# Four quarter sums in an attention kernel: standing together, or spread over v's block products

## The chip, the cores and the metric

The kernel runs on one core of a Trainium2 chip. The metric is the device time of one execution in microseconds; before the change its median over three runs is 3327.03 us (3325.53 to 3331.03). The engines are named as the profile names them: PE is TensorE (PEld its weight loads), DVE is VectorE, ACT is ScalarE, POOL is GpSimd and SP is SyncE, which issues the DMAs. Everything is in fp32.

## The reference

Two layers run one after the other on an input of 8 batches, 512 channels and 32 x 32 points (1024 tokens). Layer 0 is a group norm, an attention of 8 heads, an output projection with a second group norm, and a residual. Layer 1, in which the change lies, is an attention of one head over all 512 channels with weights normalised by row:

```python
def _L1_conv_ref(x, v_qkv, g_qkv, v_out, g_out):
    ...
    qkv = jnp.einsum('oc,bcn->bon', w_qkv, xt)
    rms = jnp.sqrt(jnp.mean(jnp.square(qkv), axis=1, keepdims=True)) + 0.0001
    qkv = qkv / rms
    q, k, v = jnp.split(qkv, 3, axis=1)
    scores = jnp.einsum('bci,bcj->bij', q, k) * C ** (-0.5)
    attn = jax.nn.softmax(scores, axis=-1)
    h = jnp.einsum('bij,bcj->bci', attn, v)
    h = jnp.einsum('oc,bcn->bon', w_out, h).reshape(B, C, H, W)
    return (x + h) * 2.0 ** (-0.5)
```

## The kernel before

The kernel loops over the 8 batches. For each it does layer 0 (`Heads`, then `finish_layer0` or, for the last batch, `finish_last`) and then layer 1 (`Layer1`, lines 739 to 907). The end of layer 1 of one batch is woven into the beginning of layer 0 of the next.

Layer 1 never forms q and k. Weights are multiplied together ahead of the loop, so that with the normalised input x of the layer the scores are x-transposed times u, where u is the product of the prepared matrix `score` with x, and v (already multiplied by the output weights) is the product of x with the prepared matrix `value`. The scale by the root mean square is put on afterwards: u's columns are multiplied by a row `rrow` on GpSimd (line 803), v's rows by `rinv` on ScalarE (line 823).

The three large products of the layer, u, v and e (the exponentials of the scores), are made by the class `Seven` (lines 607 to 689): a product of two by two blocks with seven block multiplications instead of eight (Strassen and Winograd's form). It needs, beside the blocks themselves, four sums and differences of the left operand's blocks, S1 to S4, and four of the right one's, T1 to T4. In `Seven.steps` the order of the seven is

```python
for a, b, drain in (
    (A11, "B11", c11_first),
    (S2, "T2", lambda pm: add(c["12"], c["11"], pm)),
    (S3, "T3", c22_first),
    (A22, "T4", c21),
    (S1, "T1", both),
    (S4, "B22", c12),
    (A12, "B21", c11),
):
    self.product(a, b, drain)
    yield
```

Each `product` is two matmuls of 128 contracted rows that accumulate in one PSUM bank; on the chip each fp32 matmul is two matmul instructions, so a product is four of them. Two products share one wide tile of the pool `ps_s` (three buffers of two banks each, line 101): the class variable `Seven.half` holds the second half until the next product takes it, also across units. When both halves are filled, the additions that take the two products out of PSUM ("drains", line 641) are given to VectorE, or to ScalarE for the copy `c11_first`. So additions come after every second product.

Layer 1's part of a batch, in `Layer1.project`, runs in this order: the products with `gram` and the root mean square; two units (m = 0, 1) of u's products, with x's sums T1 to T4 made on VectorE; four units of v's (line 875, each product of 256 columns); four units of e's (line 881, 512 columns). For e's the left operand is u, whose sums S1 to S4 are `s12` and `s34`, made by `sum_u` (line 830) on VectorE from u's quarters: four operations over 128 x 1024 elements. They can begin only when GpSimd has scaled u, and `sum_u` is called after v's second unit (line 877). `sum_u` also creates the tiles for the sums (pool `prob`, two buffers) and takes two of the large slots for e.

The order of the work on each engine is the order of the program text: `InOrder` (line 26) pins every instruction to it. So whatever stands ahead in an engine's queue and waits holds up what stands behind it. The tile framework adds the semaphore waits between engines. Every instruction is issued through line 34, so the profile's lines all read L34, and one tells instructions apart by their tiles. The profile leaves numbers out of tile names: `s` is `s12` or `s34` where it is next to u or in a 128x1024 addition of two tensors (it is also the name of layer 0's scores), `t` is a tile of T sums, `p_u_B`, `p_v_T`, `p_e_B` and so on are the PSUM tiles of u's, v's and e's units, named after the first letter of the right operand of the pair's first product, B or T.

Of the kernel before, what the change touches and what calls it, by code (L numbers as in the profile page):

```python
# [52 lines left out]
def attention_blocks_kernel(  # L53
# [50 lines left out]
    PE, VE, AC, PO, SY = (InOrder(tc, e) for e in (nc.tensor, nc.vector, nc.scalar, nc.gpsimd, nc.sync))  # L104

    def big(name, lead=CI):

        return slots.take([P, lead, CI * N // lead], name)
# [14 lines left out]
    def run(pieces):  # L123
        for _ in pieces:
            pass
# [95 lines left out]
    def place(name, b):  # L221
        tag, shape = places[name]
        near[name] = weights.tile(shape, F32, tag=f"w_{tag}", name=f"{name}_{b}")
        if name == "v":

            flat = near[name].rearrange("p k h c -> p (k h c)")
            near["v#"] = flat[:, CI * C :]
            near[name] = flat[:, : CI * C].rearrange("p (ci c) -> p ci c", ci=CI)
        return near[name]

    def fetch(name, b):
        SY.dma_start(out=place(name, b), in_=far[name])
# [506 lines left out]
    class Layer1:  # L739
# [10 lines left out]
        def project(self):  # L750
# [41 lines left out]
            u = self.u = big(f"u_{b}")  # L792
# [22 lines left out]
            def value_unit(m):  # L815

                w = near["value"]
                c = {f"{i + 1}{th + 1}": v[:, m + 4 * th, i * CH : (i + 1) * CH] for i in range(2) for th in range(2)}

                def last(which):  # L820
                    if which[0] == "1":
                        t = m + 4 * (which == "12")
                        AC.activation(v[:, t, :], v[:, t, :], AF.Copy, scale=rinv[:, t : t + 1])

                return Seven(
                    f"v_{b}_{m}", CH,
                    lambda k, h: w[:, k, h, :], self.right(slice(m * P, (m + 1) * P)), c, last, swap=True,
                )

            def sum_u():  # L830

                s12 = prob.tile([P, 2, 2, HN], F32, tag="p", name=f"s12_{b}")
                s34 = prob.tile([P, 2, 2, HN], F32, tag="p", name=f"s34_{b}")
                q1, q2 = halves_
                VE.tensor_add(s12[:, 0], u[:, :2, q2], u[:, 2:, q2])
                VE.tensor_sub(s12[:, 1], s12[:, 0], u[:, :2, q1])
                VE.tensor_sub(s34[:, 0], u[:, :2, q1], u[:, :2, q2])
                VE.tensor_sub(s34[:, 1], u[:, 2:, q1], s12[:, 1])
                self.s12, self.s34 = s12, s34
                for th in range(2):  # L840
                    e[th] = big(f"e_{b}_{th}", NT)
                    self.sums[th] = sum_pool.tile([P, HN], F32, tag="esum", name=f"esum_{b}_{th}")

            def weight_unit(m):

                def left(k, h):
                    if k in (A11, A12, A22):
                        return u[:, 2 * (k != A11) + h, halves_[k == A22]]  # L850
                    return {S1: self.s12[:, 0], S2: self.s12[:, 1], S3: self.s34[:, 0], S4: self.s34[:, 1]}[k][:, h, :]

                c = {f"{th + 1}{i + 1}": e[th][:, m + 4 * i, :] for i in range(2) for th in range(2)}

                def last(which):
                    th, t = int(which[0]) - 1, m + 4 * (int(which[1]) - 1)
                    et, esum = c[which], self.sums[th]
                    AC.activation(et, et, AF.Exp, bias=shift, scale=rinv[:, t : t + 1])
                    done[th].append(et)
                    if len(done[th]) == 2:  # L860
                        PO.tensor_add(esum, *done[th])
                    elif len(done[th]) > 2:
                        PO.tensor_add(esum, esum, et)

                return Seven(f"e_{b}_{m}", HN, left, self.right(slice(m * P, (m + 1) * P)), c, last, swap=True)
# [6 lines left out]
                        broadcast()  # L872
            if b + 1 < B:
                fetch("qk", b + 1)
            for m in range(4):
                run(value_unit(m).steps())
                if m == 1:
                    sum_u()
            if b + 1 < B:
                fetch("v", b + 1)  # L880
            for m in range(4):
# [139 lines left out]
    for b in range(B):  # L1021
        hn, more = heads.hn, b + 1 < B
        todo = iter(())
        for i in range(STEPS):
# [18 lines left out]
            if more:  # L1043
# [9 lines left out]
                k = i - 3 * CI - 2  # L1053
# [97 lines left out]
```

## Time and profile before

| | us |
|---|---|
| median of three runs (lowest, highest) | 3327.03 (3325.53, 3331.03) |
| the profiled execution | 3326.53 |
| its span, first to last instruction | 3324.7 |
| granted TensorE clock, mean over the span | 0.997 |
| additions into s12 and s34, 16 that read u alone | 19.5, 1218 ns each |
| the same, 8 with s first (s<-s,u) | 9.8, 1225 ns each |
| the same, 8 with s last (s<-u,s) | 9.7, 1218 ns each |
| additions into v from PSUM, 160 from p_v_T | 64.5, 420 ns each |
| additions into v from PSUM, 64 from p_v_B | 25.4, 417 ns each |
| GpSimd's scaling of u, 64 | 78.9, 1270 ns each |
| ScalarE's scaling of v, 64 | 43.6, 716 ns each |
| matmul instructions of v's products, 448 + 320 + 64 + 64 | 379 to 382 ns each |

The profile is of one execution. A page gives busy time by engine, and views of the same trace give groups of like instructions, waits, and the instructions in order of time. In the timeline a line is: start, duration, engine, line, operation, the tile written and the tiles read, shape, the number of like instructions merged, and in square brackets how long the engine was idle before it and what ended that. Matmuls overlap one another: one of 256 columns is shown with 379 ns, while 16 of them in a row start within 3.45 us. The time between starts is therefore the measure, not the sum of durations.

### The profile page before, as it was taken

To read this page: it belongs to the slowest core of one execution; us is meant where nothing else is said; L and a number is where in the kernel's file an instruction comes from. 1 tells how busy PE (TensorE), PEld (TensorE's weight loads), DVE (VectorE), ACT (ScalarE), POOL (GpSimd) and SP (SyncE) were. 2 spreads that over 40 slices of the span, in tenths; PEclk is the share of its full clock that TensorE was granted. 3 is DMA by queue.
4 is the path that set the end of the run, shared out by engine and by line. 5 is a ranking of instruction groups with operands and counts; after the bars stand their busy time and mean duration, and the time that the engine had idled before them with its cause. 6 is when DMAs were issued, how large, how long until landed. Compare 5 with 4: busy or idle time off the path is not lost.

```text
span 3324.7 us, 35644 instructions
## 1 busy us (share of the span) xinstructions
PE 3270.4 (98%) x13189; PEld 1608.1 (48%) x13189; DVE 2127.5 (64%) x2893; ACT 1069.8 (32%) x1811; POOL 981.4 (30%) x855
## 2 busy tenths in 40 slices
PE   7999999999999999999999999999999999999799
PEld 3544544445444454444544445444544445444354
DVE  4596646965479554885449754596646965478653
ACT  2353123521245212451215412254123531245210
POOL 0253123521245112450224503254123521234111
PEclk9999999999999999999999999999999999999899
DMA  5586205751068410782118811387204752067400
GB/s 187 160 212 189 76 13 155 195 176 67 7 185 209 147 45 26 204 224 95 45 50 217 236 47 44 88 216 199 76 13 142 200 166 93 5 159 203 151 7 25
DMA packets 182659, 411.86 MB, mean 124 GB/s; under 512 B 27444, under 2 KB 27480, under 8 KB 176344
## 3 DMA queue, kind: packets, MB, share of 16 engines
q1 hardware_dynamic: 182368, 409.58, 43.3%
q8 instruction: 105, 1.72, 0.2%
q14 instruction: 66, 0.54, 0.0%
q10 hardware_dynamic: 120, 0.02, 0.0%
HBM read 113.53 MB, written 27.56 MB: 42 GB/s over the span
## 4 chain that ended last, share of the span: by engine, by line
PE 86%; DVE 6%; DMA 5%; SPq 2%; issue 1%; ACT 0%; DVEq 0%; POOL 0%; POOLq 0%; ACTq 0%
PE po L34 24%; PE pqk L34 11%; PE s L34 11%; PE pv L34 7%; PE p_e_T L34 7%; PE p_e_B L34 5%; DMA pT<-pb 5%; PE py L34 4%; PE p_u_T L34 3%; PE p_o_T L34 3%; PE p_v_T L34 2%; PE p_u_B L34 2%; DVE pb L34 2%; PE p_o_B L34 2%; PE p_v_B L34 2%; SPq L34 2%
## 5 line engine op out<-in xcount | busy, mean ns | idle before, releaser
L34 ACT ACTIVATE p<-s,nm 128x1024 f32<-128x1024 f32 x512 | 565.5, 1109 | 861.3 <-DVE nm L34 825.7
L34 POOL TENSOR_SCALAR p<-p,tt 128x1024 f32<-128x1024 f32 x512 | 565.9, 1118 | 927.3 <-DVE tt L34 923.9
L34 DVE TENSOR_REDUCE nm<-s 128x1 f32<-128x1024 f32 x512 | 602.6, 1219 | 176.3 <-PE s L34 175.1
L34 DVE STREAM_TRANSPOSE pb<-p 128x2048 f32<-128x2048 f32 x256 | 589.6, 2303 | 23.2 <-POOL p L34 18.7
L34 PE MATMUL s<-qk 64*128 64x512 f32 x2048 | 508.1, 602 | 0.0
L34 PE MATMUL po<-pT,v 128*64 128x256 f32 x4096 | 470.3, 382 | 4.1 <-DMA pT<-pb 2.6
L34 PE MATMUL pqk<-hn,qk 64*128 64x512 f32 (+1 forms) x2016 | 473.9, 591 | 0.0
L34 PE MATMUL po<-e,v 128*128 128x512 f32 x1024 | 450.9, 595 | 0.0
L34 PEld LDWEIGHTS po<-pT,v 128*64 128x64 f32 x4096 | 286.7, 137 | 216.4 <-ACT v L34 71.3
L34 PEld LDWEIGHTS pqk<-hn,qk 64*128 64x128 f32 (+1 forms) x2016 | 201.8, 187 | 252.1 <-issue 239.7
L34 PEld LDWEIGHTS po<-e,v 128*128 128x128 f32 x1024 | 192.2, 190 | 252.7 <-issue 245.5
L34 POOL TENSOR_TENSOR u<-u,xy 128x512 f32<-128x512 f32 x64 | 78.9, 1270 | 781.3 <-DMA xy<-far_rinv 781.3
L34 PEld LDWEIGHTS s<-qk 64*128 64x128 f32 x2048 | 193.3, 186 | 238.6 <-issue 235.1
L34 PE MATMUL pv<-v,hn 128*128 128x512 f32 x512 | 230.7, 602 | 1.4 <-ACT v L34 1.4
L34 DVE TENSOR_TENSOR e<-e,p_e_T 128x512 f32<-128x512 f32 x160 | 107.1, 686 | 145.0 <-PE p_e_T L34 142.8
L34 POOL TENSOR_TENSOR qk<-qk,v 128x512 f32<-128x512 f32 x124 | 158.3, 1277 | 83.9 <-ACT v L34 83.9
L34 ACT ACTIVATE e<-e,shift,rinv 128x512 f32<-128x512 f32 x128 | 100.9, 811 | 247.7 <-DVE e L34 247.7
L34 POOL TENSOR_TENSOR esum<-esum,e 128x512 f32<-128x512 f32 x96 | 121.5, 1267 | 163.9 <-ACT e L34 161.4
L34 PEld LDWEIGHTS pv<-v,hn 128*128 128x128 f32 x512 | 95.3, 191 | 117.8 <-issue 116.0
L34 PE MATMUL p_e_T<-s,t 128*128 128x512 f32 x320 | 147.8, 592 | 0.0
L34 DVE TENSOR_TENSOR v<-po,esum 128x512 f32<-128x512 f32 x56 | 38.7, 691 | 160.0 <-PE po L34 159.8
L34 PE MATMUL py<-x,gram 128*128 128x512 f32 x320 | 140.7, 599 | 0.0
(184 smaller groups left out, 3077.8 us busy)
## 6 DMA issues: line engine op xcount, KB each, us to landing
pT<-pb SPq DMA_DIRECT2D x1024, 256.0 KB, 4.6
hn<-in_x_dram SPq DMA_DIRECT2D x32, 512.0 KB, 5.5
x<-in_x_dram SPq DMA_DIRECT2D x32, 512.0 KB, 5.8
out_dram<-x SPq DMA_DIRECT2D x32, 512.0 KB, 4.0
score<-far_score SPq DMA_DIRECT2D x8, 1792.0 KB, 7.5
value<-far_value SPq DMA_DIRECT2D x8, 1792.0 KB, 7.1
qk<-far_qk SPq DMA_DIRECT2D x7, 2048.0 KB, 8.1
proj<-far_proj SPq DMA_DIRECT2D x7, 1792.0 KB, 8.4
```

The source lines that it names most:

```text
L34: return lambda *args, **kw: self._pin(call(*args, **kw))
```

## The change

`sum_u` becomes a generator. Its four VectorE operations are the same, on the same tiles and in the same order, and there is a `yield` after each of the first three. The tiles and slots are made when it is first advanced. The loop over v's four units now goes through the products one by one and advances the generator after the products (unit 2, product 0), (2, 4), (3, 1) and (3, 5), counted from zero. Nothing else differs.

```diff
@@ -832,14 +832,17 @@
                 s12 = prob.tile([P, 2, 2, HN], F32, tag="p", name=f"s12_{b}")
                 s34 = prob.tile([P, 2, 2, HN], F32, tag="p", name=f"s34_{b}")
                 q1, q2 = halves_
-                VE.tensor_add(s12[:, 0], u[:, :2, q2], u[:, 2:, q2])
-                VE.tensor_sub(s12[:, 1], s12[:, 0], u[:, :2, q1])
-                VE.tensor_sub(s34[:, 0], u[:, :2, q1], u[:, :2, q2])
-                VE.tensor_sub(s34[:, 1], u[:, 2:, q1], s12[:, 1])
                 self.s12, self.s34 = s12, s34
                 for th in range(2):
                     e[th] = big(f"e_{b}_{th}", NT)
                     self.sums[th] = sum_pool.tile([P, HN], F32, tag="esum", name=f"esum_{b}_{th}")
+                VE.tensor_add(s12[:, 0], u[:, :2, q2], u[:, 2:, q2])
+                yield
+                VE.tensor_sub(s12[:, 1], s12[:, 0], u[:, :2, q1])
+                yield
+                VE.tensor_sub(s34[:, 0], u[:, :2, q1], u[:, :2, q2])
+                yield
+                VE.tensor_sub(s34[:, 1], u[:, 2:, q1], s12[:, 1])
 
             def weight_unit(m):
 
@@ -872,10 +875,11 @@
                         broadcast()
             if b + 1 < B:
                 fetch("qk", b + 1)
+            sums = sum_u()
             for m in range(4):
-                run(value_unit(m).steps())
-                if m == 1:
-                    sum_u()
+                for k, _ in enumerate(value_unit(m).steps()):
+                    if (m, k) in ((2, 0), (2, 4), (3, 1), (3, 5)):
+                        next(sums, None)
             if b + 1 < B:
                 fetch("v", b + 1)
             for m in range(4):
```

## The prediction

> **What bounds the kernel now.** I read the page first, for the share of each engine; then the list of waits of TensorE alone, because that engine is nearly always busy; then the timeline of the first batch around the four sums, TensorE and VectorE apart; last the same timeline of other batches, to see whether it repeats.
>
> ```profile
> span 3324.7 us, 35644 instructions
> PE 3270.4 (98%) x13189; PEld 1608.1 (48%) x13189; DVE 2127.5 (64%) x2893; ACT 1069.8 (32%) x1811; POOL 981.4 (30%) x855
> ```
>
> TensorE is busy for 98% of the span, so time is won only where it stands still. Its waits (who waited for whom, us in total, times, longest):
>
> ```profile
> PE pv L34 <- DVE d L34: 16.8, 5, 5.8
> PE pcol L34 <- DMA rows<-in_L_conv_b_qkv_dram: 10.6, 1, 10.6
> PE p_v_B L34 <- DVE v L34: 5.8, 8, 0.7
> ```
>
> One of them comes eight times, once per batch: v's block products wait for VectorE's additions into v. The sums are in front of those. TensorE in the first batch:
>
> ```profile
> 405.61 3.62 PE L34 MATMUL p_v_T<-value,t 128*128 128x256 f32 x16
> 409.06 2.75 PE L34 MATMUL p_v_B<-value,x 128*128 128x256 f32 x12
> 411.65 1.03 PE L34 MATMUL p_v_B<-value,t 128*128 128x256 f32 x4
> 412.51 2.75 PE L34 MATMUL p_v_T<-value,t 128*128 128x256 f32 x12
> 415.10 1.03 PE L34 MATMUL p_v_T<-value,x 128*128 128x256 f32 x4
> 416.86 1.99 PE L34 MATMUL p_v_B<-value,x 128*128 128x256 f32 x8 [0.73 <-DVE v L34]
> 418.69 3.62 PE L34 MATMUL p_v_T<-value,t 128*128 128x256 f32 x16
> 422.15 1.89 PE L34 MATMUL p_v_B<-value,x 128*128 128x256 f32 x8
> 423.87 1.88 PE L34 MATMUL p_e_B<-u,x 128*128 128x512 f32 x4
> ```
>
> and VectorE, and GpSimd's scaling of u, in the same stretch:
>
> ```profile
> 398.50 9.86 POOL L34 TENSOR_TENSOR u<-u,xy 128x512 f32<-128x512 f32 x8 [99.02 <-DMA xy<-far_rinv]
> ...
> 410.99 0.75 DVE L34 TENSOR_TENSOR v<-v,p_v_B 128x256 f32<-128x256 f32 x2 [0.52 <-PE p_v_B L34]
> 411.66 1.22 DVE L34 TENSOR_TENSOR s<-u 128x1024 f32<-128x1024 f32 x1
> 412.98 1.23 DVE L34 TENSOR_TENSOR s<-s,u 128x1024 f32<-128x1024 f32 x1
> 414.12 1.22 DVE L34 TENSOR_TENSOR s<-u 128x1024 f32<-128x1024 f32 x1
> 415.26 1.22 DVE L34 TENSOR_TENSOR s<-u,s 128x1024 f32<-128x1024 f32 x1
> 416.39 0.41 DVE L34 TENSOR_TENSOR v<-v,p_v_B 128x256 f32<-128x256 f32 x1
> 416.91 2.19 DVE L34 TENSOR_TENSOR v<-v,p_v_T 128x256 f32<-128x256 f32 x5
> ```
>
> The reader is to see the order: the four sums hold VectorE from 411.66 to 416.39, the one addition that empties the first PSUM tile of v's third unit comes behind them and ends at 416.80, and TensorE goes on at 416.86. It had run out of PSUM: the pool of wide tiles has three buffers, each takes two products (a pair), and the fourth pair of the unit needs the first pair's buffer.
>
> **The size of the hole.** A pair is 8 matmul instructions; 16 start in 409.06 - 405.61 = 3.45 us, so a pair takes 1.73 and a product 0.864. The block of 415.10 is one product, so the next was due at 415.97; it came at 416.86, 0.89 late. The block of 416.86 takes 1.83 to the next start in place of 1.73: 0.10 more. Together 0.99. Check from outside: v's products begin at 398.70 and the next stage at 423.87, 25.17 us for 28 products worth 24.18; again 0.99. The second batch (798.49 to 823.65) gives 0.98, and the timelines of the fourth and the last show the same 0.73 idle. From 423 to 830 us this idle is the only one of TensorE's matmuls in that view, so a batch is bound by TensorE from here to the same place in the next.
>
> **What the Trainium skill says.** "PSUM — Partial Sum Buffer", section "Engine vs sequencer instructions", has VectorE's queue as strictly first in, first out; the trace agrees, since the first pair was complete at about 412.7 (ScalarE's copy out of it begins at 412.71) and its addition still stood until 416.39. "VectorE: DVE Perf Modes", section on the TRN2 errata, prices an fp32 addition of two tensors at (N+151)/0.96 ns: 1224 for 1024 elements, and the trace has 1218 to 1225. "Perfetto Trace Analysis", "Optimizing Scalar/DVE Operations", says that where VectorE isn't saturated but causes bubbles elsewhere, breaking up its work can help; that is advice, and the sum below decides. "TensorE: Matmul & The Clock Gate", "What's actually happening", lets the clock fall after about 3.4 us of idleness; the hole is shorter, and the view by windows has 1.00 throughout it, so the hole costs its own length and no slower clock.
>
> **The change part by part.** No instruction is added or removed: 4 sums per batch, 32 in all, of about 1.22 us. Creating the two tiles and taking the two slots for e moves behind one product of unit 2, issues nothing, and no other slot is taken or given there. No DMA and no GpSimd instruction moves past another; only the fetch of the next batch's weights of v, which waits for v's last product, is issued as much earlier as TensorE is.
>
> Call the pairs of units 2 and 3 A to G. With no hole they start at 410.79, 412.51, 414.24, 415.97, 417.70, 419.42 and 421.15, and the stage after at 422.88. Results reach VectorE 0.20 after a pair ends (402.16 to 402.36 in unit 0). VectorE's additions per pair, as the timeline has them: A one (0.42), B two (0.88), C three (1.21), D one, E two, F three, G two (0.75). A pair's tile is needed again two pair times after the pair ended, so its additions may end 3.45 - 0.20 = 3.25 us after they became possible. The same rule gives the hole of before: A possible at 412.71, done at 416.80, 4.09, which is 0.84 too late against 0.89 measured.
>
> Now the queue with the sums spread. The first stands where it stood: behind the additions of unit 1, since unit 2's first product gives no addition until its pair is complete. It runs 411.66 to 412.88. It waits for u's scaling, which ended at 398.50 + 9.86 = 408.36: no new wait. A's addition follows ScalarE's copy (412.71 to 413.08) and ends at about 413.5. B's two: 414.44 to 415.32. Second sum: to 416.54. C's three, possible at 416.17, are 0.4 late: to 417.75. D's: 417.9 to 418.3. Third sum: to 419.5. E's: 419.6 to 420.5. F's: 421.35 to 422.56. Fourth sum: to 423.78. G's, possible at 423.08, are 0.7 late: to 424.5, where before they ended at 424.82.
>
> Against the due times: A's tile is wanted at 415.97 and free 2.4 before; C's at 419.42, 1.7 before. D's also holds the first product of unit 3, which ScalarE copies behind two scalings of v (1.33 for two): free at about 419.5, wanted at 421.15, 1.65 before. F's is free at 422.56; the weight unit takes E's tile at 422.88 and F's at 426.3. None stalls. The sums' own readers: the second is read from 424.6 (done 416.5), the third from 426.3 (419.5), the fourth, operand S4 of the sixth product, from about 431.5 (423.8). Everything that stands behind a sum has at least 1.6 us of cover; without it the sum's lateness would be TensorE's.
>
> Sum: 8 x 0.99 = 7.9 us gained, nothing added. The profiled execution took 3326.53 (span 3324.7 and 1.83 around it): 3318.6. The median of the runs is 0.5 above it: 3319.1. Bounds of what isn't shown: a scattered sum might cost the queue 1.22 or, with the spacing of dependent sums (412.98 - 411.66), 1.32; I take 1.22, and the 0.1 is inside the cover. The removed hole can give back at most 0.99 per batch, since TensorE shows no other idle there, and at least nothing. Next late, once it is gone, is TensorE itself, matmul behind matmul.
>
> **Rivals.** First, only part goes: one buffer is still late, most likely D's through ScalarE's two scalings and copy. Half the hole left is 8 x 0.5 = 4 us gained: 3323. For it: D has the longest way out, over three engines. Against: 1.65 us of cover. Chance 0.11.
>
> Second, the microsecond is won here and lost before the batch ends, because a later wait has a clock of its own (a DMA, the normalisation chains): 3327. For it: the list has waits of TensorE for VectorE's normalisation. Against: those are five in all, mostly at the start and the last batch, and none in 423 to 830. It includes the case that the instructions come out in the old order, against which stands that every engine's order is pinned to the program's. Chance 0.07.
>
> Third, slower: VectorE falls behind for good. Units 2 and 3 load it with 5.8 of additions and 4.9 of sums in 12.1 us of products. If gaps and holds raise each scattered sum to well over twice its price, say 2.9 us, 6.7 us more come in; some 2 are absorbed by its idle time (12.1 - 10.7, and the edges), 0.7 of lateness is there already, and G, F and the first tiles of the weight unit would be 5.4 late against 3.25 and one addition of 0.75: TensorE would stand 1.4 to 2.2 us per batch, about 0.8 more than the hole: 3327 + 8 x 0.8 = 3333. It decides from about 2.4 us per sum. For it: each sum now stands ahead of two or three additions. Against: nothing in the trace has a 1024-element fp32 addition over 1.23. Chance 0.05.
>
> **The numbers.** The forecast has 0.77. The range 3315.5 to 3324.0 takes in the whole hole with the runs' spread of some 3 us, and the partial case; the last two are left out. What a measurement of this kernel can tell from no change is 0.2%, 6.7 us, and my gain of 7.9 is little above it, so a good part of the forecast's own chance falls within: faster 0.60 (about three quarters of the forecast's 0.77, and a little of nothing else), same 0.33, slower 0.07 (the third rival and the spread of the second).
>
> **What would show it.** In the changed profile: the wait of p_v_B for v gone from TensorE's list; TensorE's busy time nearly the same and its span 7.9 shorter; the first p_e_B some 24.2 us after the first p_v_B of its batch; sums at about 0, 3.7, 6.6 and 10.9 us from the first one's start. A wait of TensorE in unit 3 or in the first pairs of p_e would show the step on buffers wrong; a later wait of TensorE that was not there before, the second rival; sums of over 2.4 us, the third.

## The result, and the profile after

The changed kernel takes 3319.34 us (median of nine runs, 3316.68 to 3322.0), the kernel before 3327.26 us (median of nine, 3325.53 to 3331.46). The ratio of the means is 0.9974, with a 95% interval of 0.9966 to 0.9983. By the medians it is 7.9 us faster, as forecast (3319.1); the interval allows some 6 to 11 us, so that the two medians agree to 0.3 us is in part luck, and the stages below are the closer test. The profiled execution took 3319.62 us, with a span of 3317.8.

The page of the changed kernel, its first lines, and the head of the list of TensorE's waits (who waited, for whom, us in total, times, longest):

```profile
span 3317.8 us, 35636 instructions
PE 3268.5 (99%) x13189; PEld 1609.8 (49%) x13189; DVE 2126.3 (64%) x2893; ACT 1070.7 (32%) x1811; POOL 981.4 (30%) x855
```

```profile
PE pv L34 <- DVE d L34: 16.6, 5, 5.8
PE pcol L34 <- DMA rows<-in_L_conv_b_qkv_dram: 10.3, 1, 10.3
PE po L34 <- DMA pT<-pb: 3.6, 2, 2.5
```

TensorE has as many instructions as before (so have the other engines of this line; the eight fewer in the whole count stand outside it) and nearly the same busy time, in a shorter span, and the wait of p_v_B for v, 5.8 us in eight parts, is no longer in the list. The timeline of the first batch, TensorE:

```profile
412.20 1.03 PE L34 MATMUL p_v_B<-value,t 128*128 128x256 f32 x4
413.06 2.75 PE L34 MATMUL p_v_T<-value,t 128*128 128x256 f32 x12
415.65 1.03 PE L34 MATMUL p_v_T<-value,x 128*128 128x256 f32 x4
416.51 1.89 PE L34 MATMUL p_v_B<-value,x 128*128 128x256 f32 x8
418.24 3.62 PE L34 MATMUL p_v_T<-value,t 128*128 128x256 f32 x16
421.69 1.89 PE L34 MATMUL p_v_B<-value,x 128*128 128x256 f32 x8
423.42 1.88 PE L34 MATMUL p_e_B<-u,x 128*128 128x512 f32 x4
```

and VectorE:

```profile
412.20 1.22 DVE L34 TENSOR_TENSOR s<-u 128x1024 f32<-128x1024 f32 x1
413.66 0.42 DVE L34 TENSOR_TENSOR v<-v,p_v_B 128x256 f32<-128x256 f32 x1 [0.24 <-ACT v L34]
414.99 0.87 DVE L34 TENSOR_TENSOR v<-v,p_v_T 128x256 f32<-128x256 f32 x2 [0.90 <-PE p_v_T L34]
415.78 1.22 DVE L34 TENSOR_TENSOR s<-s,u 128x1024 f32<-128x1024 f32 x1
416.92 1.20 DVE L34 TENSOR_TENSOR v<-v,p_v_T 128x256 f32<-128x256 f32 x3
418.44 0.42 DVE L34 TENSOR_TENSOR v<-v,p_v_B 128x256 f32<-128x256 f32 x1 [0.33 <-PE p_v_B L34]
418.78 1.22 DVE L34 TENSOR_TENSOR s<-u 128x1024 f32<-128x1024 f32 x1
420.24 0.88 DVE L34 TENSOR_TENSOR v<-v,p_v_T 128x256 f32<-128x256 f32 x2 [0.24 <-PE p_v_T L34]
421.89 1.21 DVE L34 TENSOR_TENSOR v<-v,p_v_T 128x256 f32<-128x256 f32 x3 [0.78 <-PE p_v_T L34]
423.02 1.22 DVE L34 TENSOR_TENSOR s<-u,s 128x1024 f32<-128x1024 f32 x1
424.15 0.74 DVE L34 TENSOR_TENSOR v<-v,p_v_B 128x256 f32<-128x256 f32 x2
```

The reader is to see that no TensorE line carries a bracket any more: 415.65 to 416.51 is 0.86 us, where the same two lines stood 1.76 apart before. VectorE still has all four sums, but the first pair's addition comes at 413.66, 1.5 us after the first sum's start and not 4.7.

The time can be accounted for by stage, from the start of the first matmul of each. From v's first product to e's first (here about 399.25 to 423.42) it is 24.17 in all eight batches of the changed kernel, and 25.17 in all eight before, each to within 0.01: 8.00 us gone. From there to the next batch's v it was 374.62 for each of the first six gaps before; after, it is 374.62 to 375.06. Four of them are a little longer, 1.2 us together, the last gap (to the last batch) is 0.66 shorter, and the first batch's v starts 0.55 later. -8.00 + 0.55 + 1.20 - 0.66 is -6.9, the difference of the two spans. The larger of the longer gaps come from layer 0: in front of its products from pT (at 692.24, where no idle time is shown, and at 1896.09, 0.19 idle) and of a product of a normalisation (2600.80, 0.22 idle); before, TensorE has no idle time in these gaps. They are most likely scatter: each of the kernels below has such longer gaps too, and with the sums at the end, slower than before, they reach 1.3 above the shortest. With one trace of each kernel it is not shown that none of the 1.2 us belongs to the change.

### The profile page after: what moved, and what is told of

Read it like the earlier page. It is cut to its first block, busy times and chain, and to the rows that moved or that the text cites. A ratio compares the mean times of both kernels' runs of the same rounds, so it can differ in the third digit from the quotient of the medians.

```text
span 3317.8 us, 35636 instructions
## 1 busy us (share of the span) xinstructions
PE 3268.5 (99%) x13189; PEld 1609.8 (49%) x13189; DVE 2126.3 (64%) x2893; ACT 1070.7 (32%) x1811; POOL 981.4 (30%) x855
## 3 DMA queue, kind: packets, MB, share of 16 engines
q8 instruction: 105, 1.72, 0.2%
## 4 chain that ended last, share of the span: by engine, by line
PE 89%; DVE 4%; DMA 4%; SPq 1%; issue 1%; ACT 0%; DVEq 0%; POOL 0%; POOLq 0%; ACTq 0%
PE po L34 25%; PE pqk L34 11%; PE s L34 11%; PE pv L34 7%; PE p_e_T L34 7%; PE p_e_B L34 5%; PE py L34 4%; PE p_u_T L34 3%; PE p_v_T L34 3%; DMA pT<-pb 3%; PE p_o_T L34 3%; PE p_v_B L34 2%; PE p_u_B L34 2%; PE p_o_B L34 2%; DVE pb L34 2%; SPq L34 1%
```

## The experiments

The theory: the hole came from VectorE's queue and the three PSUM buffers. An addition that empties a buffer may end 3.25 us after it became possible, and a sum costs nothing as long as no addition behind it is later than that. The rival: sums cost something by standing together, or by their load or their traffic. The edits of the loop are against the changed kernel. The ratios are of means, each to runs of the kernel before taken in the same session (median 3328.41 for the first four experiments, 3326.93 for the last three).

**Two and two.** The sums in two groups.

```diff
-                    if (m, k) in ((2, 0), (2, 4), (3, 1), (3, 5)):
+                    for _ in range({(2, 0): 2, (3, 1): 2}.get((m, k), 0)):
                         next(sums, None)
```

> Sums one and two after product (2, 0), three and four after (3, 1). Theory of the buffers (an addition may be 3.25 us late before TensorE runs out of PSUM): the first pair's addition ends 2.4 + 0.4 us after the sums begin, 1.4 before its buffer is due; the pair behind the second two is 1.2 early. No hole, about 3319 us, the same as the changed kernel. Rival (what costs is sums standing next to one another): about half the hole of 0.99 us per batch stays, 3323.

Measured: 3321.03 us, ratio to the kernel before 0.9976 (0.9965 to 0.9987). The median alone lies between the two expectations and its interval holds both, so the trace decides: no wait of p_v or p_e in TensorE's list, and 24.17 from v to e in all eight batches. The profiled run of 3322.69 had its excess elsewhere: from the seventh batch's e to the last batch's v it took 370.28, against 366.21 in the changed kernel's trace.

**Three and one.** `{(2, 0): 3, (3, 5): 1}` in the same line.

> Three sums after product (2, 0), the fourth after (3, 5). Theory of the buffers: the first pair's addition ends about 4.0 us after the sums begin and 0.3 before its buffer is due, so no hole, about 3319 us, and no wait of p_v_B for v; the fourth sum alone decides on the hole. Rival (each sum in front of v's additions costs its share): three quarters of the hole, 3325.

Measured: 3319.26 us, 0.9973 (0.9962 to 0.9983), no wait, 24.17 in all batches. The timeline of its first batch, VectorE and then TensorE:

```profile
409.36 1.22 DVE L34 TENSOR_TENSOR s<-u 128x1024 f32<-128x1024 f32 x1
410.69 1.23 DVE L34 TENSOR_TENSOR s<-s,u 128x1024 f32<-128x1024 f32 x1
411.83 1.22 DVE L34 TENSOR_TENSOR s<-u 128x1024 f32<-128x1024 f32 x1
412.96 0.41 DVE L34 TENSOR_TENSOR v<-v,p_v_B 128x256 f32<-128x256 f32 x1
...
412.81 1.03 PE L34 MATMUL p_v_T<-value,x 128*128 128x256 f32 x4
413.67 1.89 PE L34 MATMUL p_v_B<-value,x 128*128 128x256 f32 x8
```

The addition ends at 413.37, the pair that takes its buffer starts at 413.67, on time. Three sums together are free and the fourth costs a microsecond: a threshold, not a share for each.

**Five buffers, sums together.** The kernel before; every other pair of v's products takes one bank of the other pool.

```diff
-        half, drains = None, []
+        half, drains, turn = None, [], 0
...
+        def tile(self, name):
+            Seven.turn += 1
+            if self.width == CH and Seven.turn % 2:
+                return bank(name).rearrange("p (a f) -> p a f", a=2)
+            return wide(name)
...
-                tile_ = wide(f"p7_{self.name}_{b}")
+                tile_ = self.tile(f"p7_{self.name}_{b}")
```

> The kernel before, sums together in the middle; every other pair of v's products takes a single bank of the other PSUM pool (two products of 256 columns fill it), so that five buffers go round instead of three. Theory of the buffers: the first pair's addition still ends about 4.1 us after it became possible, but its buffer is wanted only later: no hole, about 3319 us. Rival (the sums disturb TensorE in another way, by VectorE's order or by the traffic): the hole stays, 3327.

Measured: 3318.74 us, 0.9972 (0.9961 to 0.9984), no wait, 24.17 in all batches. The first batch:

```profile
415.22 1.22 DVE L34 TENSOR_TENSOR s<-u,s 128x1024 f32<-128x1024 f32 x1
416.35 0.41 DVE L34 TENSOR_TENSOR v<-v,p_v_B 128x256 f32<-128x256 f32 x1
...
415.07 1.03 PE L34 MATMUL p_v_T<-value,x 128*128 128x256 f32 x4
415.93 1.89 PE L34 MATMUL p_v_B<-value,x 128*128 128x256 f32 x8
```

VectorE is exactly as late as in the kernel before: the addition ends at 416.76. TensorE has gone on at 415.93. With the order of before and more buffers the whole gain is there, so the buffers were the cause, and neither the sums' traffic nor their order by itself.

**Each sum twice, each three times.** In the changed kernel every sum is repeated with the same result.

```diff
-                VE.tensor_add(s12[:, 0], u[:, :2, q2], u[:, 2:, q2])
+                for _ in range(2):
+                    VE.tensor_add(s12[:, 0], u[:, :2, q2], u[:, 2:, q2])
```

and likewise for the other three, or with `range(3)`.

> The changed kernel with each sum done twice over (32 more operations of 1.22 us, 4.9 us of VectorE per batch). Theory of the buffers: the additions of the pairs are up to 3 us late, each still inside its 3.25, closest at the pair (2, 4) and (2, 5) with 0.3 to spare: 0 to 0.3 us per batch, 3319 to 3322. Rival (VectorE's load in this stretch is what counts, 12.1 us of products against 5.8 of additions and now 9.8 of sums): 3.5 us per batch, 3347 or more.

> The changed kernel with each sum done three times over (9.8 us more of VectorE per batch). Theory of the buffers, by the same sum as before: TensorE stands about 2.1 us before the pair (3, 3) and (3, 4), whose buffer waits for the three additions behind the second sum, and about 1.4 us before the first products of e, 3.6 per batch in all: 3348 us (3340 to 3356). Rival (the added load costs its length): 3319 + 78 = 3397.

Measured: twice 3317.81 us, 0.9969 (0.9958 to 0.9981), no wait; 39 us of added VectorE work cost nothing that can be measured. Three times 3350.8 us, 1.0072 (1.0055 to 1.0089). Twice, in the first batch, VectorE and TensorE:

```profile
413.77 2.48 DVE L34 TENSOR_TENSOR s<-s,u 128x1024 f32<-128x1024 f32 x2
416.17 1.20 DVE L34 TENSOR_TENSOR v<-v,p_v_T 128x256 f32<-128x256 f32 x3
...
416.10 3.62 PE L34 MATMUL p_v_T<-value,t 128*128 128x256 f32 x16
```

The three additions end at 417.37; the pair that needs their buffer is the second of the block of 416.10, at 417.83: 0.46 to spare. One place is a little closer: behind the third sum the two additions that free the buffer of e's first products end at about 420.89, and those products start at 421.28, 0.39 later. Three times, in the first batch:

```profile
420.60 1.20 DVE L34 TENSOR_TENSOR v<-v,p_v_T 128x256 f32<-128x256 f32 x3
...
418.01 1.89 PE L34 MATMUL p_v_T<-value,t 128*128 128x256 f32 x8
421.85 1.99 PE L34 MATMUL p_v_T<-value,t 128*128 128x256 f32 x8 [1.95 <-DVE v L34]
423.68 1.89 PE L34 MATMUL p_v_B<-value,x 128*128 128x256 f32 x8
426.71 1.95 PE L34 MATMUL p_e_B<-u,x 128*128 128x512 f32 x4 [1.14 <-DVE v L34]
```

The same three additions now end at 421.80, and the pair, due at 418.01 + 1.73 = 419.74, starts at 421.85: 2.11 late. e's first products are 1.30 late. Both holes are where the sum put them and nearly of its size (2.1 and 1.4). In this batch v takes 27.69, 3.52 more than 24.17; in five of the eight it is 3.90 to 3.91, for a reason given at the end. By the stages that makes about 30 us over the changed kernel.

**All four after product (2, 4), all four after (3, 6).** `{(2, 4): 4}` and `{(3, 6): 4}`.

> All four sums together after product (2, 4), in front of three additions and a scaling that TensorE's buffers depend on. Theory of the buffers: the three additions end about 1.8 us after their buffer is due, 1.9 us per batch with the slower first matmul: 3334 us, slower than before. Rival (four sums standing together cost the same wherever they stand): 3327.

> All four sums together after product (3, 6), behind all of v's additions. No buffer waits for them, but e's second product reads the second sum, which ends about 1.8 us after that product is due. If both kinds of cover count, 1.9 us per batch: 3334 us, with a wait of p_e for s in place of p_v for v. Rival (only the buffers count): 3319.

Measured: 3335.23 us, 1.0022 (1.0013 to 1.0031), and 3336.07 us, 1.0026 (1.0017 to 1.0036). Both are slower than the kernel before, by the same four operations in another place. In the middle, first batch:

```profile
419.50 1.20 DVE L34 TENSOR_TENSOR v<-v,p_v_T 128x256 f32<-128x256 f32 x3
...
420.76 1.99 PE L34 MATMUL p_v_T<-value,t 128*128 128x256 f32 x8 [1.64 <-DVE v L34]
```

and at the end:

```profile
426.48 1.23 DVE L34 TENSOR_TENSOR s<-s,u 128x1024 f32<-128x1024 f32 x1
...
424.29 1.88 PE L34 MATMUL p_e_B<-u,x 128*128 128x512 f32 x4
427.76 1.99 PE L34 MATMUL p_e_B<-s,t 128*128 128x512 f32 x4 [1.59 <-DVE s L34]
```

In the middle, three additions stand behind the sums and not one, and v takes 26.08 in place of 24.17, 1.91 more in each batch. At the end no buffer is late and v takes 24.17, but e's second product reads the second sum: due at 424.29 + 1.72 = 426.01, it starts at 427.76. So a second cover counts too, that of the sums' own readers, and it is thin at the end of v. The rival, the same cost wherever they stand together, fails in both; so does "only the buffers count".

## Why the prediction was right

The hole. It was put at 0.99 us per batch from the distance of starts, and 8 x 0.99 = 7.9. The stage from v to e became 1.00 shorter in each batch, 8.00 in all. The idle time in the bracket (0.73) would have given 5.8. It leaves out two things that the starts show: a matmul of 256 columns is shown with 379 ns where starts are 216 ns apart, so the bracket begins late, and the first pair after the hole took 1.83 to the next start in place of 1.73. The distance of starts was the right measure.

The queue with the sums spread. The four sums were forecast at 0, 3.7, 6.6 and 10.9 us from the first; they stand at 0, 3.58, 6.58 and 10.82. C's additions were forecast 0.4 late and G's 0.7; C's, possible at 415.65 + 0.86 + 0.20 = 416.71, start at 416.92, and G's, possible at 423.42 + 0.20 = 423.62, at 424.15: 0.2 and 0.5. Neighbouring operations on VectorE start slightly before the one ahead has ended (416.92 against 415.78 + 1.22 = 417.00), which the sum left out.

The cover. The 3.25 us were taken from one pair's rhythm and checked on one hole. Three sums in front of an addition left 0.30 us by the trace of that experiment, 0.3 by the expectation; four sums pass it by 0.84, worked out, and 0.89, measured. Five buffers made the cover larger and the hole went without the change.

First rival, a partial gain through ScalarE's longer way out of pair D: it did not come. ScalarE's copy, as the timeline of the changed kernel has it, was done by 419.87 (419.52 + 0.35) and the buffer was wanted at 421.69, 1.82 later where the forecast had 1.65. Second rival, the gain lost later: the bulk of it is out, since at most the 1.2 us of longer gaps could be such a loss, and the last gap gave 0.66 back. One of their places is a normalisation, which this rival named; whether a little of the gain is lost there stays open. Third rival, VectorE behind for good: its deciding point was put at about 2.4 us per sum. Doubled sums held the queue for 2.40 us each (413.77 to 416.17) and left 0.39 us at the closest place; tripled ones, 3.66 (416.94 to 420.60), made two holes. The point lies between, and the change, with 1.22 per sum, stands at half of it or less.

The profiled execution came out at 3319.62 and not 3318.6: the 1.0 us are the small terms of the accounting by stage, at the start and in the gaps, which the sum did not contain.

No kernel here beats the changed one beyond the scatter of the runs: the versions without a hole have medians of 3317.81 to 3321.03 and the same 24.17 in every batch.

## What to carry to other kernels

VectorE's side work here cost nothing by its length (39 us more of it were free) but by what it made late (the same four sums in other places cost 8 or 16 us). So count the buffers in the ring, take the time of the turns between a tile's completion and its reuse, and keep every run of side work in front of an evacuation below that; then check the same for the readers of that work. One hole of a microsecond, where it recurs in every batch, is seen best as the distance between starts of the bound engine, compared with the same block elsewhere. Splitting in four was more than needed here (three and one, or two and two, are equal), but it leaves room for twice the work.

## What the runs showed that was not expected

The prediction took from the Trainium skill ("TensorE: Matmul & The Clock Gate", "What's actually happening") that the clock falls after about 3.4 us of idleness, so that a hole of 1 us is free of it. Up to 1.64 us idle (sums in the middle) the view by windows of 15 us around the hole indeed has 1.00 in all eight batches. With the sums three times over, the hole of 1.95 us was followed by a fall of the clock in five of the eight, so here the measurement decides against reading the page's figure as the shortest idle time that counts. The third batch of that kernel, its timeline and its windows (stretch: length, busy time of each engine with its instructions, then the granted clock, the DMA share and GB/s):

```profile
1226.71 3.68 PE L34 MATMUL p_v_T<-value,t 128*128 128x256 f32 x8 [1.95 <-DVE v L34]
```

```profile
1225.00:1227.00 2.00, 0.29 (x1) 0.29 (x2) 1.97 (x6) 0.31 (x1) 0.00 (x0) 0.96 0.00 0
1227.00:1229.00 2.00, 2.00 (x6) 1.55 (x6) 1.97 (x2) 1.28 (x3) 0.00 (x0) 0.50 0.00 0
1229.00:1231.00 2.00, 2.00 (x8) 1.65 (x7) 1.94 (x3) 0.00 (x0) 0.00 (x0) 0.68 0.00 0
1231.00:1233.00 2.00, 2.00 (x9) 1.39 (x8) 1.86 (x5) 0.00 (x0) 0.00 (x0) 1.00 0.03 8
```

The clock is at half for about 3.4 us (worked out from 0.96, 0.50 and 0.68 over 2 us each: what is missing from 1.00, 0.08 + 1.00 + 0.64 us, is half of that), and the eight matmuls take 3.68 us in place of 1.99. Most of it fell into the second hole, so the batch lost only 0.38 more (28.07 from v to e, against 27.69 in the first batch). Why the clock stayed at 1.00 in the other three batches was not tried.

The second surprise is where the traces differ. In the nine traces v's first product starts between 396.41 and 400.12 us, and from the seventh batch's e to the last batch's v it takes 366.21 to 370.28 (the sums at the end left aside, where a hole lies in e), while v and e themselves repeat to 0.01 us within each kernel where the clock holds and TensorE doesn't wait. So these nine traces differ at the start and in the last batch's layer 0 by up to some 4 us, apart from the stretch that was changed. That the scatter of some 5 us between runs of one kernel comes from the same places is likely, but not shown: each kernel has one trace.
